# Layer 1's row statistics on ScalarE instead of VectorE, and an older split of the copies that prepare layer 0's weights

## The chip, the cores and the metric

The kernel runs on one core of one Trainium2 chip. Five engines of the core work side by side, each with its own instruction stream: TensorE (PE in the profile; PEld is its weight load), VectorE (DVE), ScalarE (ACT), GpSimd (POOL) and SyncE (SP, which here only issues DMAs). The metric is the device time of one execution in microseconds (us). The kernel before takes 5475.15 us, the median of three runs (5474.11 to 5475.48).

## What is computed

Four graph layers follow one another over a batch of 128 graphs with 128 nodes and 512 features; after each layer the input is added and every row is normalised. The change touches two of them. Cut to what matters:

```python
def _layernorm(x, axis=-1, eps=1e-5):
    m = jnp.mean(x, axis=axis, keepdims=True)
    v = jnp.var(x, axis=axis, keepdims=True)
    return (x - m) / jnp.sqrt(v + eps)

# layer 0 (its weights Wv, aw, Wk are prepared once, at the start of the kernel)
Xw = X @ Wv + bv
sj = Xw @ aw[:d, 0]
si = Xw @ aw[d:, 0]
...
for k in range(Wk.shape[0]):               # 3 steps
    H = H + Xk @ Wk[k] + bk[k]
    Xk = jnp.einsum('bij,bjd->bid', transition, Xk)

# layer 1: 128 graphs x 128 nodes, hidden width 1024
h = jax.nn.relu(hypergraph_conv(x, adj, W1, b1))     # rows of 1024
h = layer_norm(h, gamma, beta)                       # mean and variance of each row of 1024
y = hypergraph_conv(h, adj, W2, b2)
return y + x
```

Layers 2 and 3 (a tanh graph attention and an eight-head attention) are not touched.

## The kernel before

All the instructions of the kernel are first written into a plan. Each gets a key (the place in time it should have), an estimated duration and its dependences; a list scheduler in the host code then fixes the order of the instructions on every engine, and only then are they emitted. So every instruction has the same source line (L369) in the profile, and groups are told apart by tile names. The scheduler takes TensorE's instructions by key, and the others by the time at which TensorE needs them. An engine executes its instructions strictly in the order that was fixed, so a change of a few instructions gives a new order for everything behind it.

The weight products are two-level Strassen products: seven blocks for each of seven blocks. In layer 1 an inner product (`strassen` with `nk=1`) writes seven 256-column results, and each of them has to be read out of its PSUM bank before the bank is used on. Five of the seven inner products are read by VectorE alone (`biased_take`), two by ScalarE and VectorE (`plain_take`):

```python
def biased_take(dst, bias, scale=None):
    def op(d, b, u):
        if scale is None:
            return lambda p: ve.tensor_tensor(d, p, b, OP.add)
    ...
def plain_take(d11, d12, d21, d22):
    add = ve.tensor_tensor
    return {
        "p1": lambda p: ac.copy(d11, p), "c11": lambda p: add(d11, p, d11, OP.add),
        "v": lambda p: ac.copy(d12, p), "c12": lambda p: add(d12, p, d12, OP.add),
        "p5": lambda p: ac.copy(d22, p), "c22": lambda p: add(d22, p, d22, OP.add),
        "c21": lambda p: ac.copy(d21, p),
    }
```

The rows of 1024 are finished like this, once for each of the 128 graphs (128 partitions are the graph's nodes, 1024 elements lie along the free axis, in two halves `g`):

```python
def stats(st, k, piece):
    ve.bn_stats(st[:, 6 * k:6 * k + 6], piece)

def norm_terms(st, n=1):
    mv = col(2)
    ve.bn_aggr(mv, st[:, :6 * n])
    ve.tensor_scalar(mv[:, 1:2], mv[:, 1:2], EPS, None, op0=OP.add)
    ve.tensor_scalar(mv[:, 0:1], mv[:, 0:1], -1.0, None, op0=OP.mult)
    rstd = col(1)
    po.tensor_tensor(rstd, mv[:, 1:2], neghalf, OP.pow)
    nmr = col(1)
    ac.mul(nmr, mv[:, 0:1], rstd)
    return nmr, rstd
...
# in layer1, for each graph
ve.scalar_tensor_tensor(t, t, dns[r][b], rows1[:, :2]..., op0=OP.mult, op1=OP.add)
ac.activation(t, t, AF.Relu)
sts = col(12)
for g in range(2):
    stats(sts, g, h[r][b][:, g])
nmr, rstd = norm_terms(sts, 2)
ac.activation(t, t, AF.Identity, bias=nmr, scale=rstd)
loads.append(through_dram(...))     # written to DRAM and read back turned
```

`norm_terms` also serves the rows of 512 that end every layer; those are not changed.

The preparation of layer 0's weights, at the very start: the twelve transfers of `Wk`'s first half go through ScalarE's own DMA queue, Wv is transposed by TensorE, and the score columns `Wv @ aw` are taken from the transposed copy:

```python
for g in range(2):
    for m in range(3):
        with plan.together():
            for k in range(4):
                (ac, sp)[g].dma_start(stage[m]..., wk0[m]...)      # g=0: on ScalarE's queue
...
wvT = [four() for _ in range(2)]
for j in range(C):                                                 # C = 4
    pt = bank()
    ... pe.transpose(...) x4
    ve.tensor_copy(wvT[j // 2][:, j % 2]..., pt...)
two = fixed(C, 2, name="cols0")
p = bank()
... pe.matmul(p[:, 2 * c:2 * c + 2], wvT[...], awc...) x32         # Wv @ aw
ac.copy(two.rearrange("p c k -> p (c k)"), p[:, :2 * C])
for g, half, j in ((0, 0, B11), (1, 0, B21), (0, 1, B12), (1, 1, B22)):
    for m in range(3):
        (ac.copy, ve.tensor_copy)[g](W[j]..., stage[m]...)         # 128x512 each
    ...
    combine(W[j], (ve, po)[half])          # four subtractions of 386 columns
combine_once_more(W, (T3, N4))             # four subtractions of 2702 columns
```

Of the kernel before, what the change touches and what calls it, by code (L numbers as in the profile page):

```python
# [13 lines left out]
AF = mybir.ActivationFunctionType  # L14
OP = mybir.AluOpType
AX = mybir.AxisListType

P = 128
D = 512
C = D // P  # L20
Q = 32
DH = 1024
# [3 lines left out]
EPS = 1e-5  # L26
# [1 line left out]
BUFS = 12  # L28
SQS = 8
COLS = 32  # L30
ROWS = 4
KS = 4
OUTS = 4

# [343 lines left out]
def kernel(  # L378
# [57 lines left out]
    def fixed(*shape, name, kind="fixed"):  # L436
        t = const.tile([P, *shape], FP, name=name)
        return View(Tile(kind, t), np.arange(math.prod(shape)).reshape(shape))
# [11 lines left out]
    def col(*n):  # L450
        return tile_of("col", *n)
# [4 lines left out]
    neghalf = fixed(1, name="neghalf")  # L456
    po.memset(neghalf, -0.5)
    tiny = fixed(1, name="tiny")
    po.memset(tiny, 1e-12)
    junk = fixed(D, name="junk", kind="free")  # L460

    def dot(dst, u, v, n=D):
        ve.scalar_tensor_tensor(junk[:, :n], u, 1.0, v, op0=OP.mult, op1=OP.mult, accum_out=dst)
# [172 lines left out]
# [13 lines that stand above are left out]
# [164 lines left out]
    def prepare0():  # L813
        h = D // 2
# [27 lines left out]
        for j in range(C):  # L842
            pt = bank()
            with plan.together():
                for c in range(C):
                    pe.transpose(pt[:, c * P:(c + 1) * P], st[c // 2][:, c % 2, j * P:(j + 1) * P], ident)

            ve.tensor_copy(wvT[j // 2][:, j % 2].rearrange("p (c k a) -> p k c a", k=4, a=Q),
                                             pt.rearrange("p (k c a) -> p k c a", k=4, a=Q))
        two = fixed(C, 2, name="cols0")  # L850
        p = bank()
# [6 lines left out]
        ac.copy(two.rearrange("p c k -> p (c k)"), p[:, :2 * C])  # L858
        for g, half, j in ((0, 0, B11), (1, 0, B21), (0, 1, B12), (1, 1, B22)):
            for m in range(3):  # L860
                (ac.copy, ve.tensor_copy)[g](W[j][:, :4, :, m * P:(m + 1) * P].rearrange("p (n c) o i -> p c n (o i)", n=2), stage[m].rearrange("p c (n i) -> p c n i", i=P)[
                    :, 2 * g:2 * g + 2, 2 * half:2 * half + 2])
            scores = W[j][:, :4, 0, 3 * P:]
            if half:
                po.memset(scores, 0.0)
            else:
                po.memset(scores[:, 2:], 0.0)
                ac.copy(scores[:, :2], two[:, 2 * g:2 * g + 2])
            combine(W[j], (ve, po)[half])
        combine_once_more(W, (T3, N4))  # L870
        p = bank()
# [135 lines left out]
    def layer1(i0):  # L1007
# [66 lines left out]
        for r, i in enumerate(both):  # L1074
            plan.key = base + STEP1 * (5, 7)[r]
            for b in range(U):
                t = h[r][b].rearrange("p g f -> p (g f)")
                ve.scalar_tensor_tensor(t, t, dns[r][b], rows1[:, :2].rearrange("p g f -> p (g f)"),
                                        op0=OP.mult, op1=OP.add)
                ac.activation(t, t, AF.Relu)  # L1080
                sts = col(12)
                for g in range(2):
                    stats(sts, g, h[r][b][:, g])
                nmr, rstd = norm_terms(sts, 2)
                ac.activation(t, t, AF.Identity, bias=nmr, scale=rstd)
                loads.append(through_dram(h[r][b].rearrange("p (j g) (k w) -> p j (g k) w", j=1, k=2), f"h{i + b}"))
        for r, i in enumerate(both):
# [296 lines left out]
```

## Time and profile before

| | |
|---|---|
| span of the profiled execution | 5473.7 us |
| instructions | 94041 |
| TensorE busy | 5349.7 us (98%) |
| VectorE busy | 4551.0 us (83%) |
| GpSimd busy | 4041.0 us (74%) |
| ScalarE busy | 2392.4 us (44%) |
| two DVE groups on the rows of 1024: statistics of one half, aggregation | 681 ns, 199 ns mean |

How to read it. Busy shares are averages over the whole span; the layers lie one behind the other and have different limits, so the shares of a stretch say more than these. "Idle before" of a group is the time that its engine stood still just before the group's instructions, with the engine whose instruction ended most of it. The tile names tell the use: `bank` and `t` are PSUM, `first` is the large area that holds layer 0's weights at first and the rows of 1024 in layer 1 (128x1024, or 128x512 for a half), `col` the small per-row numbers.

### The profile page before, as it was taken

To read this page: it belongs to the slowest core of one execution; us is meant where nothing else is said; L and a number is where in the kernel's file an instruction comes from. 1 tells how busy PE (TensorE), PEld (TensorE's weight loads), DVE (VectorE), ACT (ScalarE), POOL (GpSimd) and SP (SyncE) were. 2 spreads that over 40 slices of the span, in tenths; PEclk is the share of its full clock that TensorE was granted. 3 is DMA by queue.
4 is the path that set the end of the run, shared out by engine and by line. 5 is a ranking of instruction groups with operands and counts; after the bars stand their busy time and mean duration, and the time that the engine had idled before them with its cause. 6 is when DMAs were issued, how large, how long until landed. Compare 5 with 4: busy or idle time off the path is not lost.

```text
span 5473.7 us, 94041 instructions
## 1 busy us (share of the span) xinstructions
PE 5349.7 (98%) x29145; PEld 4259.2 (78%) x29145; DVE 4551.0 (83%) x11561; ACT 2392.4 (44%) x6471; POOL 4041.0 (74%) x4835
## 2 busy tenths in 40 slices
PE   8999999999999999999999999999999999999998
PEld 4555555555788888888888789999999999999987
DVE  6788888878998899998889978778878777878876
ACT  2444343434434434443434344444455445445444
POOL 6666666666777777877777567777777777777776
PEclk8999999999999999999999999999999999999999
DMA  3333333334454545545445545554555554555553
GB/s 93 104 98 98 101 101 102 94 103 129 145 150 144 155 144 148 155 148 152 147 148 150 161 129 165 161 162 154 162 162 156 162 163 151 162 166 159 160 154 119
DMA packets 788381, 768.35 MB, mean 140 GB/s; under 512 B 264859, under 2 KB 592547, under 8 KB 787878
## 3 DMA queue, kind: packets, MB, share of 16 engines
q1 hardware_dynamic: 786374, 759.71, 45.8%
q8 instruction: 231, 3.78, 0.3%
q10 hardware_dynamic: 1504, 2.62, 0.2%
q14 instruction: 272, 2.23, 0.1%
HBM read 435.83 MB, written 326.24 MB: 139 GB/s over the span
## 4 chain that ended last, share of the span: by engine, by line
PE 57%; DVE 7%; DMA 3%; POOL 1%; issue 1%; ACT 1%; SPq 1%; DVEq 0%; POOLq 0%; ACTq 0%
PE bank L369 43%; PE t L369 15%; DVE first L369 2%; DVE col L369 2%; DVE out L369 1%; DVE four L369 1%; SPq L369 1%; POOL out L369 1%; DMA h<-first 1%; DMA out<-h 1%; ACT first L369 0%; DVE junk L369 0%; DMA first<-x3d 0%; POOL first L369 0%; POOL four L369 0%
## 5 line engine op out<-in xcount | busy, mean ns | idle before, releaser
L369 PE MATMUL bank<-first,four 128*128 128x386 f32 (+3 forms) x5176 | 1437.1, 431 | 37.2 <-DVE out L369 14.8
L369 PEld LDWEIGHTS bank<-first,four 128*128 128x128 f32 (+2 forms) x5176 | 847.7, 187 | 592.9 <-DVE out L369 139.0
L369 DVE TENSOR_TENSOR out<-bank,out 128x386 f32<-128x386 f32 (+1 forms) x1884 | 928.1, 510 | 282.4 <-PE bank L369 223.3
L369 POOL TENSOR_TENSOR out<-out 128x256 f32<-128x256 f32 (+3 forms) x482 | 550.4, 1152 | 300.6 <-DVE out L369 210.0
L369 POOL TENSOR_TENSOR col<-col,neghalf 128x1 f32<-128x1 f32 x640 | 380.6, 600 | 377.8 <-DVE col L369 376.2
L369 DVE TENSOR_TENSOR first<-bank,first 128x256 f32<-128x256 f32 x1362 | 543.6, 414 | 130.2 <-PE bank L369 100.6
L369 PE MATMUL bank<-first,out 128*128 128x256 f32 (+2 forms) x2560 | 624.0, 382 | 26.4 <-DVE first L369 9.4
L369 PEld LDWEIGHTS bank<-first,out 128*128 128x128 f32 (+1 forms) x2560 | 469.2, 190 | 128.7 <-DVE first L369 30.8
L369 PE MATMUL bank<-four,out 128*128 128x256 f32 (+2 forms) x2118 | 538.4, 376 | 2.2 <-DVE col L369 1.4
L369 DVE TENSOR_TENSOR four<-bank,four 128x256 f32<-128x256 f32 x818 | 338.4, 418 | 142.1 <-PE bank L369 127.5
L369 PE MATMUL bank<-out,first 128*128 128x128 f32 (+2 forms) x2840 | 427.9, 290 | 0.9 <-DVE out L369 0.4
L369 ACT COPY out<-bank 128x258 f32<-128x258 f32 (+2 forms) x555 | 236.7, 431 | 436.8 <-PE bank L369 388.6
L369 PEld LDWEIGHTS bank<-four,out 128*128 128x128 f32 (+2 forms) x2118 | 369.8, 189 | 58.5 <-issue 8.4
L369 PEld LDWEIGHTS bank<-out,first 128*128 128x128 f32 (+1 forms) x2840 | 374.5, 188 | 24.7 <-DVE four L369 2.8
L369 ACT ACTIVATE col<-col,col 128x1 f32<-128x1 f32 x640 | 183.2, 292 | 456.4 <-POOL col L369 388.2
L369 POOL TENSOR_TENSOR four<-four,four 128x256 f32<-128x256 f32 (+2 forms) x395 | 328.8, 837 | 14.4 <-DVE col L369 4.8
L369 ACT COPY t<-out 128x512 f32<-128x512 f32 x256 | 150.2, 591 | 421.1 <-DVE four L369 248.8
L369 POOL TENSOR_TENSOR first<-first 128x512 f32<-128x512 f32 (+3 forms) x196 | 234.4, 1208 | 105.5 <-DVE first L369 67.4
L369 POOL TENSOR_TENSOR four<-four 128x256 f32<-128x256 f32 (+2 forms) x331 | 245.4, 758 | 66.9 <-DVE four L369 36.3
L369 POOL TENSOR_TENSOR out<-out,out 128x256 f32<-128x256 f32 (+2 forms) x286 | 287.2, 1008 | 9.3 <-DVE four L369 4.5
L369 POOL TENSOR_SCALAR sq<-sq,col 128x128 f32<-128x128 f32 x256 | 160.7, 638 | 148.8 <-DVE col L369 146.5
L369 DVE BATCH_NORM_STATS2 col<-first 128x6 f32<-128x512 f32 x370 | 245.7, 681 | 26.9 <-ACT first L369 25.1
(407 smaller groups left out, 12718.5 us busy)
## 6 DMA issues: line engine op xcount, KB each, us to landing
h<-first SPq DMA_DIRECT2D x496, 128.0 KB, 2.4
out<-x1d SPq DMA_DIRECT2D x88, 512.0 KB, 4.5
out<-h SPq DMA_DIRECT2D x87, 512.0 KB, 4.6
four<-in_x_dram SPq DMA_DIRECT2D x512, 64.0 KB, 2.0
four<-in_x_dram SPq DMA_DIRECT2D x62, 512.0 KB, 3.6
x1d<-four SPq DMA_DIRECT2D x62, 512.0 KB, 2.7
first<-S SPq DMA_DIRECT2D x61, 512.0 KB, 4.4
out<-S SPq DMA_DIRECT2D x50, 512.0 KB, 4.4
```

The lines of the kernel that those rows point to most:

```text
L369: call(*map(real, args), **{n: real(a) for n, a in kw.items()})
```

## The change

Layer 1's rows get their mean from the accumulator that the relu can write as it goes, and their variance from two squares on ScalarE, each of which also writes the sum along its half. With `mean` holding minus the sum over 32 times 1024, a square computes (h/32 + mean) squared, so that the two sums together are the variance. Three small VectorE instructions make the numbers from these, and the product of mean and factor moves from ScalarE to VectorE. VectorE's statistics and their aggregation fall away for these rows. The purpose is to take work off VectorE in layer 1.

The same diff takes back an arrangement in the preparation of layer 0's weights: two of the four copies of the transposed Wv go from VectorE to ScalarE, and so do six copies of Wk's blocks. The pool of rows of 512 is cut from four buffers to two, which makes room for a scratch tile for the squares' outputs.

```diff
-ROWS = 4
+ROWS = 2
...
+    junk_act = fixed(D, name="junk_act", kind="free")
...
-            ve.tensor_copy(wvT[j // 2][:, j % 2].rearrange("p (c k a) -> p k c a", k=4, a=Q),
+            (ve.tensor_copy, ac.copy)[j % 2](wvT[j // 2][:, j % 2].rearrange("p (c k a) -> p k c a", k=4, a=Q),
...
-                (ac.copy, ve.tensor_copy)[g](W[j][:, :4, :, m * P:(m + 1) * P]...
+                ac.copy(W[j][:, :4, :, m * P:(m + 1) * P]...
...
-                ac.activation(t, t, AF.Relu)
-                sts = col(12)
+
+                total, mean, var, rstd, nmr = col(1), col(1), col(2), col(1), col(1)
+                ac.activation(t, t, AF.Relu, accum_out=total)
+                ve.tensor_scalar(mean, total, -1 / (32 * DH), None, op0=OP.mult)
                 for g in range(2):
-                    stats(sts, g, h[r][b][:, g])
-                nmr, rstd = norm_terms(sts, 2)
+                    ac.activation(junk_act, h[r][b][:, g], AF.Square, bias=mean, scale=1 / 32, accum_out=var[:, g:g + 1])
+                ve.tensor_scalar(var[:, :1], var[:, :1], var[:, 1:], EPS, op0=OP.add, op1=OP.add)
+                po.tensor_tensor(rstd, var[:, :1], neghalf, OP.pow)
+                ve.tensor_scalar(nmr, mean, rstd, 32.0, op0=OP.mult, op1=OP.mult)
                 ac.activation(t, t, AF.Identity, bias=nmr, scale=rstd)
```

More of the change, by code (lines that the diff above doesn't have):

```diff
@@ L860, in prepare0 @@
             for m in range(3):
-                (ac.copy, ve.tensor_copy)[g](W[j][:, :4, :, m * P:(m + 1) * P].rearrange("p (n c) o i -> p c n (o i)", n=2), stage[m].rearrange("p c (n i) -> p c n i", i=P)[
+                ac.copy(W[j][:, :4, :, m * P:(m + 1) * P].rearrange("p (n c) o i -> p c n (o i)", n=2), stage[m].rearrange("p c (n i) -> p c n i", i=P)[
                     :, 2 * g:2 * g + 2, 2 * half:2 * half + 2])
```

## The prediction

> **What bounds the kernel now.** I read the page's busy shares first, then busy time in windows of 100 us to find the layers, then the waits of TensorE inside layer 1, then single groups, and last the timeline of the first 60 us. TensorE is busy 98% of the span, so the question is only where its last 2% lie. Layer 1 runs from about 1330 to 3100 us (the writes of its rows to DRAM start at 1386 us and end at 3101); layers 2 and 3 come behind it. Two windows, one in the middle of layer 1 and one in the middle of layers 2 and 3; the columns are length, then busy us of each engine with its instructions, clock, DMA share and GB/s:
>
> ```profile
> core 0: us, PE busy (x) PEld busy (x) DVE busy (x) ACT busy (x) POOL busy (x), PEclk, DMA share, GB/s
> 1300.00:1500.00 200.00, 183.15 (x820) 140.95 (x821) 186.80 (x457) 82.11 (x161) 155.84 (x188) 0.97 0.51 151
> 1500.00:3000.00 1500.00, 1472.56 (x7027) 1238.26 (x7026) 1353.46 (x3362) 610.71 (x1149) 1162.87 (x1360) 1.00 0.50 148
> 3300.00:5200.00 1900.00, 1896.86 (x14099) 1734.50 (x14096) 1522.96 (x4036) 943.02 (x3222) 1479.21 (x1820) 1.00 0.52 160
> ```
>
> In layers 2 and 3 VectorE is busy 80% (1522.96 of 1900), ScalarE 50%, GpSimd 78%, and TensorE stands still for 3.1 us of 1900. In layer 1 VectorE is busy 90%, ScalarE 41%, GpSimd 78%, and TensorE stands still for 27.4 us of 1500. The entry, 1300 to 1500, loses another 16.9 us with VectorE at 93%. What TensorE waits for in 1500 to 3000 (total us, times, longest), matmuls and weight loads:
>
> ```profile
> PE bank L369 <- DVE col L369: 11.4, 11, 2.0
> PE bank L369 <- DVE first L369: 6.7, 15, 0.9
> PE t L369 <- DVE col L369: 3.1, 3, 1.8
> PE t L369 <- DVE first L369: 2.8, 8, 0.7
> PE bank L369 <- ACT four L369: 2.3, 3, 0.9
> ```
>
> ```profile
> PEld bank L369 <- DVE first L369: 38.1, 77, 1.3
> ```
>
> 24.0 of the 26.9 us of matmul waits are ended by VectorE: late evictions (`first`) and work queued in front of them (`col`). The weight loads wait for VectorE far oftener, 77 times here and 34 times (16.8 us) into the other PSUM tiles, in pieces of 0.5 us in the mean; part of each is hidden by the matmul still running. So layer 1 is TensorE-bound with VectorE close behind, and VectorE's queue is what ends TensorE's pauses.
>
> **What the Trainium skill says.** "Perfetto Trace Analysis", Identifying the Most-Contended Engine, says that matmul busy time is no good measure of how near TensorE is to its limit. The trace agrees: stretches of layer 1 that all read 97 to 99% busy do 459 to 480 matmuls in 100 us. I therefore use the count as well. "ScalarE: Activation LUTs", What ACT_TABLE_LOAD costs, gives an ACTIVATE with a pointer bias about 280 ns + 0.833 ns per element, with 93 ns of overlap between neighbours. The slope agrees here: (1240 - 813) / 512 = 0.834 ns from the Identity on 1024 and on 512 columns. The same page, Table sets: the hidden batching unit, says that a function outside the loaded set needs a reload; the trace has one table load (1283 ns) in the whole kernel, and no run yet shows a Square. "GPSIMD Engine Reference", Specifications, says that GpSimd shares its SBUF interfaces with VectorE and collides with VectorE instructions of two SBUF inputs. The statistics have one input, so taking them away should shorten GpSimd's work little. The collision itself is in the trace: the 128x1024 scalar_tensor_tensor takes from 1220 to 4655 ns.
>
> **The change part by part.** The groups of 1500 to 3000 give VectorE's costs (busy us, mean ns), and a stretch of layer 3's timeline gives the spacing of activations that write a sum:
>
> ```profile
> L369 DVE BATCH_NORM_STATS2 col<-first 128x6 f32<-128x512 f32 x218 | 143.0, 681 | 22.6 <-ACT first L369 22.3
> ...
> L369 DVE TENSOR_SCALAR col<-col 128x1 f32<-128x1 f32 x440 | 48.9, 143 | 1.5
> ...
> L369 DVE BATCH_NORM_AGGREGATE col<-col 128x2 f32<-128x12 f32 x110 | 21.9, 199 | 1.1
> ```
>
> ```profile
> 4022.76 0.41 ACT L369 ACTIVATE first<-first,col 128x128 f32<-128x128 f32 x1
> 4023.05 0.21 ACT L369 ACTIVATION_READ_ACCUMULATOR first<-first,col 128x1 f32 x1
> 4023.15 0.41 ACT L369 ACTIVATE first<-first,col 128x128 f32<-128x128 f32 x1
> ```
>
> VectorE, per graph. Removed: two statistics of 143.0/218 = 0.656 us, one aggregation of 0.199, two small instructions of 48.9/440 = 0.111, together 1.73 us. Added: three small instructions, two of them with pointer operands; I take 0.14 us each, 0.42 us. Net -1.31 us, times 128 graphs -168 us. Spread over the 1770 us of layer 1 that is 9.5 points, so VectorE goes from 90% to about 81%.
>
> ScalarE, per graph. An activation of 128 columns with its sum follows the last after 0.39 us; 384 further columns at 0.834 ns make 0.32, so a Square of 512 costs about 0.71 us, two 1.42. The relu's sum costs the part of the read that doesn't overlap, 4023.15 minus 4023.05, 0.10. The product for nmr goes, 0.29 (its mean is 292 ns). Net +1.23 us, times 128 is +157 us, 9 points: ScalarE from 41% to about 50%.
>
> GpSimd keeps its one power per row. The latency of one row changes little: 1.3 us of statistics become 1.4 us of squares, and a step through VectorE is added where one through ScalarE is removed. It has slack anyway: the plan wants a row's statistics between 1.1 and 1.5 steps into the stage and its read-back at 2.4 to 3.0, and one step is 28 us (1770 / 64).
>
> After the change layer 1 has the same shares as layers 2 and 3 have now (VectorE 80%, ScalarE 50%, GpSimd 78%), whose inner products have the same seven evictions. That is my main ground: TensorE's idle time per 100 us should fall from 1.8 us towards the 0.17 us there. By the count, the best undisturbed 100 us of layer 1 (2100 to 2200) holds 480 matmuls; 7027 at that rate would take 1464 us in place of 1500, so 36 us are to be had there, 42 us over 1770. I take 60% of that, 25 us, since some of the stalls come from the mixture of work and from the order rather than from load. At the entry (16.9 us idle, VectorE 93%) about 10 us are ended by VectorE; I take 4 of them, because layer 1's first rows come only late in it.
>
> The preparation, from the timeline of the first microseconds (start, length, engine; idle before in brackets):
>
> ```profile
> 11.02 4.65 PEld L369 LDWEIGHTS bank<-aw_c,four 128*128 128x128 f32 x32
> ...
> 17.47 1.28 ACT L369 ACT_TABLE_LOAD   x1 [17.47 <-DMA first<-in_L_gnn_Wk_dram]
> ...
> 22.03 0.16 ACT L369 COPY cols<-bank 128x8 f32<-128x8 f32 x1
> ...
> 22.23 1.84 DVE L369 TENSOR_TENSOR first<-first 128x386 f32<-128x386 f32 x2 [8.84 <-ACT cols L369]
> ```
>
> ScalarE issues DMAs until 17.4 us and can compute only from 18.8. The two Wv copies that move to it were done on VectorE by 11.1 us; there they end at about 20. The 32 score products (4.7 us) then run from 20 to 24.7, the copy of the columns comes at 24.8 in place of 22.03, and VectorE's first subtraction is some 2.7 us later. Against it, VectorE loses six Wk copies, 1.22 + 0.88 + 1.33 = 3.4 us, in a stretch (20 to 40 us) where it is busy 17.4 of 20 and sets TensorE's pauses, and ScalarE, busy 4 of 20, has room for them. I book 0, give or take 3.
>
> The row pool has four users in the whole kernel, and the later two start long after the first two have ended: 0. Sum: -25 - 4 + 0 = -29, and a point of pessimism for the reordering of stages that already lose almost nothing. 5475 - 28 = 5447 us.
>
> **The rivals.** First: ScalarE becomes the new late one. In layer 1 it evicts 22 results per four graphs, and an eviction that arrives behind two squares and an Identity waits 1.4 + 1.24 us. Against it: layers 2 and 3 run rows of eight exponentials (over 3 us without a break) at the same load with TensorE idle 0.17%. For it: 2.3 us of waits on `ACT four` exist already at 41%. If it holds, half of the gain is lost: 5460 us.
>
> Second: the stalls aren't VectorE's load but its order. An eviction is due about 0.4 us after its matmul, and any 1.2 to 1.7 us instruction in front of it (transposes, scalar_tensor_tensor) makes it late; the statistics at 0.66 us are the smaller obstacles. Then only their share counts: perhaps 10 us, 5465 us.
>
> Third: the new order, with nothing of the mechanism, moves other stages by chance. Layer 0 (from 100 to 1200 us) idles 4 us in all and layers 2 and 3 scarcely, so they can only lose; I give this 10 us either way.
>
> Fourth: Square needs a table reload. Layer 1 uses only Relu, Identity, Copy and Square, so one set could serve throughout it, and the cost would be a few loads at the borders, under 10 us; only alternating loads would cost hundreds, and I give that 1%.
>
> **Range and chances.** The centre is 5447. Full success (42 + 10, with a lucky preparation) makes 5423, the first two rivals 5460 to 5465, with the third on top 5475. I take 5430 to 5466 for eight in ten. A gain of 2% would be 109 us, more than twice what layer 1 loses, so it needs something I don't see: 1.5%. A loss of 2% needs table reloads or a broken order: 1%.
>
> **What would show it.** In the windows of layer 1 VectorE near 81%, ScalarE near 50%, TensorE's idle time under 10 us in 1500 of its middle, and more than 475 matmuls per 100 us; the waits on `DVE first` and `DVE col` more than halved; in ScalarE's groups 256 Squares of about 0.7 us busy and still one table load; the score columns copied near 24.8 us but layer 0 at full pace at about the same time as before. I am wrong if the VectorE waits shrink and ScalarE's grow by as much (first rival), or if VectorE falls to 81% and its waits stay (second), or if the time moves outside layer 1.

## The result, and the profile after

| | median us | runs (lowest to highest) | ratio to before, 95% interval |
|---|---|---|---|
| before | 5474.63 | 4 (5472.12 to 5475.48) | |
| after | 5506.34 | 4 (5496.10 to 5514.32) | 1.0058 [1.0038, 1.0077] |

The change costs 31.7 us where I predicted a gain of 28. The profiled run is the fastest of the four; its span is 5494.3 us, so the trace accounts for 20.6 of these 31.7 us and is silent on the rest.

First the busy times in windows, the same columns as before. The third window is the passage from layer 1 to layer 2.

```profile
core 0: us, PE busy (x) PEld busy (x) DVE busy (x) ACT busy (x) POOL busy (x), PEclk, DMA share, GB/s
1300.00:1500.00 200.00, 180.01 (x811) 139.37 (x811) 171.74 (x438) 93.40 (x198) 156.08 (x186) 0.95 0.48 146
1500.00:3000.00 1500.00, 1465.43 (x7014) 1238.30 (x7012) 1269.88 (x3131) 755.91 (x1588) 1178.97 (x1360) 1.00 0.50 148
3000.00:3300.00 300.00, 273.52 (x1534) 232.69 (x1535) 249.29 (x590) 126.95 (x333) 183.53 (x208) 0.97 0.49 151
3300.00:5200.00 1900.00, 1890.20 (x14000) 1720.49 (x13998) 1513.64 (x4005) 925.21 (x3182) 1470.38 (x1807) 1.00 0.52 158
```

The relief is there: in the middle of layer 1 VectorE falls from 90.2% to 84.7% and ScalarE rises from 40.7% to 50.4%. TensorE doesn't profit. It stands still for 34.6 us in place of 27.4 and gets 7014 matmuls done in place of 7027. And in layers 2 and 3, which the change doesn't touch, 14000 matmuls fit where 14099 did; at their pace of 7.42 a microsecond that is 13 us.

What TensorE's matmuls wait for between 1500 and 3000 us (total us, times, longest):

```profile
PE bank L369 <- ACT first L369: 29.0, 26, 1.2
PE bank L369 <- DVE first L369: 1.9, 5, 0.5
PE t L369 <- DVE first L369: 1.7, 3, 0.8
```

VectorE ended 24.0 us of these waits before and ends 3.6 now. In their place stands one wait that wasn't there, for ScalarE, 26 times with some 1.1 us each: once in every group of four graphs (layer 1 has 32 such groups, and this window holds about 27). The timeline around one of them, with start, length and engine; I left out what lies between:

```profile
1998.83 0.72 ACT L369 ACTIVATE junk_act<-first,col 128x512 f32<-128x512 f32 x1
...
1999.68 0.72 ACT L369 ACTIVATE junk_act<-first,col 128x512 f32<-128x512 f32 x1
...
2002.13 0.20 DVE L369 TENSOR_SCALAR col<-col,col 128x1 f32<-128x1 f32 x1
...
2002.38 1.24 ACT L369 ACTIVATE first<-first,col,col 128x1024 f32<-128x1024 f32 x1 [1.88 <-DVE col L369]
...
2002.85 1.77 DVE L369 SCALAR_TENSOR_TENSOR four<-rows,col 128x512 f32<-128x512 f32 x1
...
2004.54 0.15 DVE L369 TENSOR_SCALAR col<-bank 128x2 f32<-128x2 f32 x1
...
2004.72 0.38 ACT L369 COPY ks<-bank 128x260 f32<-128x260 f32 x1 [0.85 <-DVE col L369]
...
2005.00 0.38 ACT L369 COPY first<-bank 128x256 f32<-128x256 f32 x1
...
2005.52 0.67 PE L369 MATMUL bank<-first,out 128*128 128x256 f32 x2 [1.03 <-ACT first L369]
```

Read it from the bottom. TensorE stops for 1.03 us because the eviction at 2005.00 came late. ScalarE wasn't busy then: it stood at the head of its queue with a copy of K (`ks<-bank`), the node-by-node product of two of layer 1's graphs, which waits for VectorE to read the same PSUM bank first (`col<-bank`), and VectorE was held up by a scalar_tensor_tensor of 1.77 us. Before that, ScalarE had waited 1.88 us for `nmr`, which the change moved from ScalarE to VectorE. So this isn't load but waiting at the head of an in-order queue. ScalarE's waits show how common it is (total us, times, longest); before, `first` waited for VectorE's small results 22.6 us and `ks` 10.6, and there was no `junk_act`:

```profile
ACT first L369 <- DVE col L369: 68.5, 54, 1.9
ACT junk_act L369 <- DVE col L369: 45.2, 54, 1.4
ACT ks L369 <- DVE col L369: 43.7, 41, 2.0
```

The costs of the added instructions, ScalarE's and then VectorE's groups of the same window (busy us, mean ns | idle just before):

```profile
L369 ACT ACTIVATE junk_act<-first,col 128x512 f32<-128x512 f32 x220 | 158.9, 722 | 48.8 <-DVE col L369 45.2
L369 ACT ACTIVATE first<-first,col,col 128x1024 f32<-128x1024 f32 x109 | 135.5, 1243 | 58.9 <-DVE col L369 57.5
...
L369 ACT ACTIVATION_READ_ACCUMULATOR junk_act<-first,col 128x1 f32 x220 | 41.1, 187 | 0.0
```

```profile
L369 DVE TENSOR_SCALAR col<-col 128x1 f32<-128x1 f32 x440 | 64.1, 161 | 48.1 <-ACT first L369 30.7 <-ACT junk_act L369 14.7
```

The preparation and the passage to layer 2, from the timeline:

```profile
19.52 6.71 PE L369 MATMUL bank<-aw_c,four 128*128 128x2 f32 x30 [6.30 <-ACT four L369]
...
26.27 0.17 ACT L369 COPY cols<-bank 128x8 f32<-128x8 f32 x1 [4.24 <-PE bank L369]
...
3140.19 1.23 DVE L369 STREAM_TRANSPOSE out<-four 128x1024 f32<-128x1024 f32 x1
...
3141.53 2.05 PE L369 MATMUL bank<-first,out 128*128 128x256 f32 x4 [12.88 <-issue]
```

The score columns come at 26.27 us; I had expected 24.8. At 3141 TensorE has stood for 12.9 us; the profile names nothing that ended this wait, but VectorE's transpose into `out` ended just before it. Almost all of it comes back: against the same matmul of the kernel before, after lags by 5.9 us at matmul 12100, 15.7 at 12200 and 5.7 at 12700.

To see where time goes I compare two traces by TensorE's matmuls done: when was the n-th finished? Matmul 3500 ends at 1208 us of the kernel before, ahead of layer 1; 13000 at 3276 us, behind the passage to layer 2; 28500 at 5369 us. After lags by 2.2 us at the first, 6.3 at the second, 21.9 at the third. So the preparation and layer 0 cost 2.2 us, layer 1 with its passage 4.2 (I had predicted -29), and layers 2 and 3 cost 15.5 (I had predicted 0).

### The profile page after: what moved, and what is told of

Read it like the earlier page. It is cut to its first block, busy times and chain, and to the rows that moved or that the text cites. A ratio compares the mean times of both kernels' runs of the same rounds, so it can differ in the third digit from the quotient of the medians.

```text
span 5494.3 us, 94155 instructions
## 1 busy us (share of the span) xinstructions
PE 5347.4 (97%) x29145; PEld 4258.8 (78%) x29145; DVE 4451.9 (81%) x11297; ACT 2559.9 (47%) x6991; POOL 4059.3 (74%) x4835
## 4 chain that ended last, share of the span: by engine, by line
PE 55%; DVE 9%; DMA 4%; ACT 2%; issue 2%; SPq 2%; POOL 1%; DVEq 0%; ACTq 0%; POOLq 0%
PE bank L369 42%; PE t L369 12%; DVE out L369 3%; DVE first L369 2%; DVE col L369 2%; SPq L369 2%; DVE four L369 1%; ACT first L369 1%; DMA out<-x1d 1%; DMA out<-h 1%; DMA sq<-in_adj_dram 1%; ACT junk_act L369 1%; DVE junk L369 0%; DMA out<-x3d 0%; DMA four<-x1d 0%
## 5 line engine op out<-in xcount | busy, mean ns | idle before, releaser
L369 PE MATMUL bank<-first,four 128*128 128x386 f32 (+3 forms) x5184 | 1497.9, 437 | 23.4 <-DVE out L369 10.9
L369 PE MATMUL bank<-first,out 128*128 128x256 f32 (+2 forms) x3214 | 770.4, 379 | 51.5 <-ACT first L369 29.5
L369 PEld LDWEIGHTS bank<-first,out 128*128 128x128 f32 (+1 forms) x3214 | 585.3, 189 | 174.0 <-issue 65.7
L369 DVE TENSOR_TENSOR four<-bank,four 128x256 f32<-128x256 f32 x1094 | 447.8, 417 | 203.2 <-PE bank L369 189.6
L369 DVE TENSOR_TENSOR first<-bank,first 128x256 f32<-128x256 f32 x1179 | 477.0, 415 | 130.1 <-PE bank L369 93.2
L369 POOL TENSOR_TENSOR first<-first 128x512 f32<-128x512 f32 (+4 forms) x237 | 250.7, 1069 | 185.5 <-DVE first L369 146.4
L369 PE MATMUL bank<-four,out 128*128 128x256 f32 (+2 forms) x1354 | 343.4, 372 | 2.7 <-DVE first L369 1.7
L369 POOL TENSOR_TENSOR four<-four 128x256 f32<-128x256 f32 (+1 forms) x342 | 244.9, 734 | 61.4 <-DVE four L369 40.7
L369 ACT COPY four<-bank 128x256 f32<-128x256 f32 (+1 forms) x245 | 108.8, 448 | 330.2 <-PE bank L369 323.5
L369 PE MATMUL t<-out,sq 128*128 128x512 f32 x512 | 259.9, 595 | 0.6 <-DVE sq L369 0.4
L369 PEld LDWEIGHTS bank<-four,out 128*128 128x128 f32 (+2 forms) x1354 | 228.4, 185 | 41.1 <-DVE first L369 10.3
```

The lines of the kernel that those rows point to most:

```text
L369: call(*map(real, args), **{n: real(a) for n, a in kw.items()})
```

## The experiments

The plan's own part in this has to be told first. It orders everything once, and then up to twice more with deadlines taken from the order before; I call what it writes after one and after two of these steps the first and second order. It keeps the one with the earlier end by its own estimate. For the kernel before these ends are 5363.67 and 5364.69 us and it emits the first order; for after 5359.26 and 5356.73, and it emits the second. So a change of a few instructions also switches the order of 94,000, on an estimate that is 0.05% lower.

Theory A is that the loss lies in the change itself: its row statistics pass between the queues of the engines seven times (VectorE, ScalarE, VectorE, ScalarE, VectorE, GpSimd, VectorE, ScalarE) where they passed four times, and every pass is a chance to block a queue. Theory B is that the order decides. Theory C is ScalarE's load, theory D the preparation.

All 18 runs, and the change itself, in one table. Each ratio is to the kernel before as it was measured again beside that run; its medians there lay between 5473.7 and 5479.6 us, so medians of runs that were not measured together compare only to some 5 us. "Layer 1" is what a run gains (-) or loses against the kernel before between matmul 3500 and matmul 13000, "layers 2, 3" between 13000 and 28500, each from one profiled run; e1, which does in layer 1 what after does, differs from after by 2 and 1 us there, so differences of a few us say nothing. Ahead of matmul 3500 the runs lag by -1 to 10 us, which is in neither column.

| run | median us | ratio, 95% interval | layer 1 | layers 2, 3 |
|---|---|---|---|---|
| after | 5506.3 | 1.0058 [1.0038, 1.0077] | +4.2 | +15.5 |
| e1 after, old preparation | 5506.0 | 1.0053 [1.0038, 1.0068] | +6.5 | +16.9 |
| e2 before, new preparation | 5479.8 | 1.0003 [0.9995, 1.0012] | -1.5 | -0.2 |
| e3 after, first order | 5472.2 | 0.9992 [0.9983, 1.0001] | -14.2 | +3.8 |
| e4 before, second order | 5491.7 | 1.0028 [1.0019, 1.0038] | -4.1 | +13.5 |
| e5 after, K copy later | 5527.8 | 1.0093 [1.0078, 1.0108] | +29.9 | +16.2 |
| e6 after, no squares, first order | 5480.6 | 1.0006 [0.9999, 1.0012] | -5.4 | +6.6 |
| e7 before, third order | 5493.4 | 1.0028 [1.0017, 1.0040] | -6.2 | +21.7 |
| e8 after, third order | 5500.2 | 1.0044 [1.0029, 1.0059] | +8.1 | +17.1 |
| e9 after, K copy sooner | 5498.0 | 1.0036 [1.0024, 1.0049] | +2.7 | +20.3 |
| e10 after, one SBUF input | 5505.1 | 1.0043 [1.0030, 1.0055] | +10.6 | +18.3 |
| e11 before, slack 50 | 5469.5 | 0.9983 [0.9975, 0.9990] | -23.4 | +11.0 |
| e12 after, slack 50 | 5489.6 | 1.0021 [1.0015, 1.0028] | -5.7 | +11.2 |
| e13 no pass through VectorE | 5458.4 | 0.9973 [0.9962, 0.9984] | -21.4 | +1.5 |
| e14 the same, slack 50, second order | 5487.1 | 1.0023 [1.0014, 1.0031] | -11.4 | +15.7 |
| e15 before, nmr on VectorE | 5477.3 | 1.0007 [0.9999, 1.0015] | -1.1 | +0.4 |
| e16 one VectorE step | 5497.2 | 1.0039 [1.0025, 1.0053] | +8.9 | +13.6 |
| e17 e13 in the second order | 5469.7 | 0.9985 [0.9978, 0.9991] | -24.5 | +17.7 |
| e18 e13, slack 50, first order | 5502.3 | 1.0043 [1.0029, 1.0057] | +14.4 | +9.2 |

**e1 and e2: which half of the change.** e1 is after with the preparation of before, e2 is before with the preparation of after and the smaller row pool.

```diff
 # e1
-            (ve.tensor_copy, ac.copy)[j % 2](wvT...
+            ve.tensor_copy(wvT...
-                ac.copy(W[j]...
+                (ac.copy, ve.tensor_copy)[g](W[j]...
 # e2: the same lines the other way round in before, and ROWS = 2
```

> The changed kernel with the preparation of the kernel before: only layer 1's statistics are moved. If the preparation's copies carry the loss, this is at or below 5475 us. If the loss comes from layer 1 and what follows (the main theory: VectorE's waits are gone, 24 us, but one wait of about 1.1 us on ScalarE for each of the 32 groups of four graphs, 35 us, has come in their place), it stays near the changed kernel, 5490 to 5512 us, with the start some 2 us earlier.

> The kernel before with only the preparation (and the row pool of 2) of the changed one. Lag at the start of the full pace in the changed kernel was about 2 us, so if nothing else depends on it 5477 us; if the preparation carries the loss, 5490 us or more.

Measured: e1 at 1.0053 loses all that after loses, e2 at 1.0003 nothing that can be told from zero. Theory D is out.

**e3 and e4: the same work in the other order.**

```diff
 # e3, in after: one step of deadlines
-    def emit(self, places, rounds=2):
+    def emit(self, places, rounds=1):
 # e4, in before: always take the later order
-            if other[2] < end:
+            if True:
```

> The changed kernel, but the plan emits its first order by deadlines and not the second one, which it took since its own estimate was lower by 0.05%; the kernel before was emitted in its first one. The instructions are the same ones. If the loss is the order's (what happens to stand in front of what), the time moves by more than 10 us, perhaps below 5475; if it is the work's (Squares on ScalarE), it stays within 5 us of the changed kernel and the waits on ScalarE in layer 1 stay at about 29 us in 1500 to 3000.

> The kernel before in its second order by deadlines, which it had turned down (its own estimate was higher by 0.02%). If orders of the same work differ by tens of us, this moves by more than 10 us; if the order matters little, 5475 within 5 us.

Measured: after in the first order takes 5472 us, 34 less than the same instructions in the second, so the whole loss is gone with the work unchanged. TensorE's waits for ScalarE's `first` in 1500 to 3000 are 4.0 us there in place of 29.0, the longest 0.3. Before in the second order takes 5492, 17 more. The windows of e4, in the middle of layer 1 and of layers 2 and 3:

```profile
1500.00:3000.00 1500.00, 1473.14 (x7035) 1240.56 (x7034) 1344.31 (x3368) 611.67 (x1148) 1170.99 (x1359) 1.00 0.50 149
3300.00:5200.00 1900.00, 1891.90 (x13995) 1719.73 (x13994) 1510.47 (x3999) 925.36 (x3184) 1469.26 (x1804) 1.00 0.52 159
```

In the second line the old work loses the same hundred matmuls (13995 against 14099) as after did, with the shares of the engines hardly changed: what after lost in layers 2 and 3 is the order's and not the change's. The matmuls' own waits there are only 8.1 us; the weight loads show the rest of it in part. The four largest groups of their waits for VectorE come to 10.9 us in before in this stretch, and to 28.9 us in e4:

```profile
PEld bank L369 <- DVE out L369: 14.2, 38, 1.6
PEld bank L369 <- DVE four L369: 7.0, 30, 0.6
PEld bank L369 <- DVE first L369: 5.0, 13, 1.1
PEld bank L369 <- DVE ks L369: 2.7, 10, 1.1
```

**e5 and e9: is the copy of K what blocks ScalarE's queue?** Both take after's order and move only this copy. e5 issues it behind the two evictions that follow; some of the copies then read a bank that the next product had overwritten, which changes the numbers but not the work. e9 issues it in front of VectorE's read of the same bank.

```diff
-        for k in sorted(range(len(start)), key=...):
+        for k in self.k_later(sorted(range(len(start)), key=...)):            # e5
+        for k in self.k_sooner(sorted(range(len(start)), key=...), place):    # e9
```

> The changed kernel in its own (second) order, with one thing moved: ScalarE's copy of K out of PSUM, which stands behind a VectorE instruction that reads the same bank, goes behind the two evictions that TensorE waits for. Theory (that copy, waiting for VectorE, blocks ScalarE's queue and so makes the evictions late, 29 us in 1500 to 3000, about 33 in all of layer 1): the waits on ACT first in 1500 to 3000 fall from 29 to under 6 us and the time falls from about 5506 by 20 to 33 us. Rival (the Squares and the Identity in front of them make the evictions late): waits and time stay within 8 us.

> The changed kernel in its own (second) order, with every engine's sequence as it is, but ScalarE's copy of K is issued in front of VectorE's first read of the same PSUM bank, so that VectorE waits for ScalarE there and not ScalarE for VectorE. In the changed kernel 62 of the 64 copies of K wait for VectorE; here 5 do. If that wait is what makes ScalarE's evictions late: TensorE's waits on ACT first in 1500 to 3000 fall from 29 us to under 8, and the time falls by 15 to 30 us, to 5475 to 5490. If the Identity and the Squares in front do it: no change within 6 us.

Measured: e5 was a miss. The copy now stood behind a later VectorE read of the bank, where it waited 1.46 us in every second group of graphs (0.80 in the others) in place of 0.85, and in front of other evictions. TensorE's wait for ScalarE stayed (31.5 us, 26 times), and the kernel lost some 20 us more. In e9 every engine's queue holds the same instructions in the same order as in after, but for five of ScalarE's 6991 places; what differs is who waits for whom at this bank. Of the 64 copies 47 wait for a semaphore of VectorE in after, and 3 in e9. What TensorE waits for in e9 between 1500 and 3000 (the line number differs, since the helper is longer):

```profile
PE bank L400 <- DVE first L400: 14.0, 35, 0.7
PE t L400 <- DVE first L400: 3.1, 8, 0.6
PE bank L400 <- ACT first L400: 3.1, 13, 0.2
```

The wait for ScalarE fell from 29.0 to 3.1 us, which shows that the blocked copy caused it. But half of it came back as waits for VectorE (17.1 us against 3.6), in 43 pieces of at most 0.7 us, and the weight loads' waits for VectorE's `first` doubled (57.5 us against 28.2). TensorE's idle time fell from 34.6 to 23.0 us, yet it did 7022 matmuls in the window in place of 7014, and layer 1 costs 2.7 us in place of 4.2. The median is 8 us lower, with intervals that overlap, where I had expected 15 to 30. So the blocked copy is what TensorE was seen to wait for; that it is what layer 1 lost isn't shown.

**e6: theory C, ScalarE's load.** Without the squares; the variance's place is taken by a number without meaning, so the rows get another scale; the squares are all that is left out. First order, to be compared with e3.

```diff
-                for g in range(2):
-                    ac.activation(junk_act, h[r][b][:, g], AF.Square, bias=mean, scale=1 / 32, accum_out=var[:, g:g + 1])
-                ve.tensor_scalar(var[:, :1], var[:, :1], var[:, 1:], EPS, op0=OP.add, op1=OP.add)
+                ve.tensor_scalar(var[:, :1], total, mean, EPS, op0=OP.add, op1=OP.add)
```

> The changed kernel in the plan's first order, without the two Squares (a number made of the row's sum stands for the variance, so the rows are scaled wrongly): VectorE is relieved and ScalarE gets nothing for it. If the Squares on ScalarE take away part of the gain, this is well under the changed kernel's first order (5472), 5460 or less. If the gain is bounded by how evictions stand in VectorE's queue, it is within 6 us of 5472.

Measured:

```profile
1500.00:3000.00 1500.00, 1479.75 (x7073) 1245.89 (x7073) 1242.53 (x3160) 595.99 (x1154) 1143.16 (x1371) 1.00 0.51 150
```

ScalarE falls to 39.7%, below what it had before the change, and VectorE is at 82.8%. Yet TensorE still idles 20.3 us, and the run is not faster than e3, which does all the squares (1.0006 against 0.9992). As the cause of the loss, theory C is out. Since e6 too has an order of its own, an effect of ScalarE's load smaller than the tens of us between orders can't be excluded. And with VectorE relieved and ScalarE not burdened at all, layer 1 gains 5 us: relief alone wasn't worth 29 here.

**e7, e8, e11, e12: two further orders of both kernels.** The third order takes three steps of deadlines; the slack is a constant of the plan's scheduler.

```diff
-    def emit(self, places, rounds=2):
+    def emit(self, places, rounds=3):      # e7 before, e8 after; the last order is always taken
-SLACK = 60
+SLACK = 50                                 # e11 before, e12 after; both plans take the first order
```

> The kernel before in its third order by deadlines. The first gave 5477 and the second 5492. A third value some 10 us from either would show that an order is worth as much as the change; together with the changed kernel's third order it gives a third pair that differs in the work alone.

> The changed kernel in its third order by deadlines. If the change of work is worth 10 to 15 us in layer 1 as in the first order, 10 to 15 us under the kernel before in its third order; if the Squares cost as much as the statistics did, equal or above, and waits on ScalarE in layer 1 of 20 us or more come back.

> The kernel before with the plan's slack at 50 in place of 60 (how far ahead of the readiest instruction it may pick by rank): the same instructions in one more order. By the three orders so far, 5477 to 5493.

> The changed kernel with the slack at 50: a fourth pair. If the change itself is worth the 4 us of the first pair, it is near the kernel before with this slack, within 8 us; if the new waits on ScalarE go with the change in most orders, as in two of three, it is 7 to 30 us above.

Measured: in pairs of the same setting, after against before is -0.08% (first), +0.30% (second), +0.16% (third) and +0.38% (slack 50), in the ratios of the table. The change loses in three orders of four; the first pair can't be told apart. In layer 1 alone, by the table, it is worth -14, +8, +14 and +18 us in these pairs, so the sign is the order's. The most telling run is e11, which has the old statistics on VectorE:

```profile
1500.00:3000.00 1500.00, 1484.24 (x7106) 1251.86 (x7106) 1346.95 (x3388) 621.23 (x1160) 1178.83 (x1380) 1.00 0.50 150
```

VectorE is as busy as before, 89.8%, and TensorE does 7106 matmuls in place of 7027 and idles 15.8 us in place of 27.4. Layer 1 gains 23 us, most of what I had meant to win by relieving VectorE, with no relief at all. Of the changed kernel's orders, e8 has the once-per-group wait for ScalarE again (25.7 us, 23 times). In e12 such a wait is there, too, but on the other engine:

```profile
PE bank L369 <- DVE first L369: 27.3, 25, 1.9
```

**e10: does a collision of VectorE and GpSimd start the stall?** The 1.77 us instruction that held up VectorE in the timeline adds b2 from a second SBUF operand. e10 leaves that addition out and reads one operand (the form it uses also writes a sum, which adds a read of some 0.08 us).

```diff
+                if self.ops[k][0] == DVE and ...:     # rows * factor + b2
+                    nc.vector.tensor_scalar(to, u, s, None, op0=OP.mult, op1=OP.add, accum_out=spare)
```

> The changed kernel in its own order, but VectorE's product of bw2 and the row number, 128x512, doesn't add b2 (which is zero), so it has one SBUF input and can't collide with GpSimd: 0.99 us should become about 0.65 us. At the place of the wait it stretches to 1.77 us beside GpSimd's 128x512 subtractions, in front of VectorE's read of K's bank. If that delay starts the chain (VectorE late, ScalarE's copy of K late, eviction late), TensorE's waits on ACT first fall from 29 us to under 12 and the time by 15 to 30 us. If it doesn't, within 8 us of the changed kernel.

Measured: 1.0043, and the wait for ScalarE is still 26.3 us, 26 times. But the delay has only moved. The two instructions that stand in front of VectorE's read of K's bank took 0.68 and 1.77 us in after (2002.26 and 2002.85); at such a place of e10 they are

```profile
2005.29 1.58 DVE L372 SCALAR_TENSOR_TENSOR four<-out,four 128x512 f32<-128x512 f32 x1
2006.79 0.73 DVE L1364 TENSOR_SCALAR_CACHE_REDUCE four<-rows,col 128x512 f32<-128x512 f32 x1
```

The changed instruction takes 722 to 748 ns throughout e10, whatever GpSimd does. Its neighbour, which still has two SBUF operands (`four<-out,four` and `out<-out,out`), takes up to 687 ns where GpSimd stands still, and 1311 ns in the mean, up to 1797, where GpSimd works all the while. So the collision is real, and e10 didn't take it away; whether it starts the stall stays open.

**e13, e14, e17, e18: theory A by itself.** All row statistics on ScalarE and GpSimd, with no pass through VectorE between the relu and the Identity: one square over 1024 elements, and the factor 32 that is left over goes into W2.

```diff
-                ve.tensor_scalar(mean, total, -1 / (32 * DH), None, op0=OP.mult)
-                for g in range(2):
-                    ac.activation(junk_act, h[r][b][:, g], AF.Square, bias=mean, scale=1 / 32, accum_out=var[:, g:g + 1])
-                ve.tensor_scalar(var[:, :1], var[:, :1], var[:, 1:], EPS, op0=OP.add, op1=OP.add)
-                po.tensor_tensor(rstd, var[:, :1], neghalf, OP.pow)
-                ve.tensor_scalar(nmr, mean, rstd, 32.0, op0=OP.mult, op1=OP.mult)
+                ac.mul(mean, total, -1 / DH)
+                ac.activation(junk_act, t, AF.Square, bias=mean, accum_out=var)
+                ac.activation(var, var, AF.Identity, bias=eps1)          # eps1 holds 1024 * EPS
+                po.tensor_tensor(rstd, var, neghalf, OP.pow)
+                ac.mul(nmr, mean, rstd)
```

The plan takes the first order for it at slack 60 (e13) and the second at slack 50 (e14). e17 and e18 are the two that are missing: second order at 60, first at 50.

> The changed kernel with the whole of layer 1's row statistics off VectorE: ScalarE also scales the sum, squares all 1024 columns in one instruction, adds eps and forms nmr (rows stay a factor of 32 small, W2 is loaded 32 times larger). A row then goes VectorE, ScalarE, GpSimd, ScalarE, and VectorE's queue holds nothing that waits for ScalarE. ScalarE does about as much as in the changed kernel. Theory A (VectorE's queue is held up by small instructions that wait for ScalarE and GpSimd, 55 us in 1500 to 3000 of the changed kernel against 22 before, and evictions stand behind them): VectorE's waits for ScalarE and GpSimd in the chain are gone, layer 1 gains 15 us or more on the kernel before, the time is 5450 to 5465. Theory B (layer 1 loses by the order alone): anything between 5465 and 5500, with a wait once in each group of four graphs.

> The same work as the last with the plan's slack at 50, another order, to be held against the kernel before with that slack (5469) and the changed kernel with it (5490). Theory A: 10 us or more under the kernel before, 5445 to 5460. Theory B: no steady sign against the other kernels.

> The row statistics wholly on ScalarE and GpSimd, as in the run of 5458 us, but in the plan's second order (the one that the changed kernel has). If the passages between the engines' queues cost the changed kernel its gain, this one beats it in the same order by 10 to 20 us in layer 1, as it did in the first order (14 us): 5485 to 5497 us, about the 5492 of the kernel before in its second order or below. If only the order counts, it comes out where the changed kernel is: 5500 to 5512.

> The same statistics with the other slack (50 for 60), but in the plan's first order, as the kernels before and after with that slack have it (5469 and 5490 us); the 5487 us measured of it were in the second order. If the passages count: below the changed kernel's 5490 by 15 us or more, so 5455 to 5475. If only the order counts, anything from 5470 to 5490, with no gain in layer 1 beyond that of the changed kernel.

Measured: e13 takes 5458.4 us and beats both kernels, 0.27% below before [0.9962, 0.9984]. ScalarE's groups show that the waiting for VectorE in front of squares and Identity is gone (48.8 and 58.9 us of idle time in after's lines above, next to 3.5 and 0.9 here):

```profile
L369 ACT ACTIVATE first<-first,col,col 128x1024 f32<-128x1024 f32 x110 | 136.1, 1237 | 0.9
L369 ACT ACTIVATE junk_act<-first,col 128x1024 f32<-128x1024 f32 x110 | 126.4, 1149 | 3.5
```

e17 speaks for theory A most clearly. In the second order the version without the passes takes 5469.7 us, where after takes 5506.3 and before 5491.7; that is more than I expected of it. Its windows:

```profile
1500.00:3000.00 1500.00, 1475.37 (x7086) 1251.79 (x7087) 1232.88 (x2838) 790.17 (x1701) 1135.63 (x1379) 1.00 0.51 150
...
3300.00:5200.00 1900.00, 1890.63 (x13980) 1716.68 (x13979) 1512.08 (x4002) 925.21 (x3183) 1471.62 (x1807) 1.00 0.52 159
```

Layer 1 gains 24 us, and layers 2 and 3 lose what every second order loses. But e18 is a miss, and it limits what theory A may claim. (So is e14, with 5487 us where theory A had 5445 to 5460; no run has the old work or the change in its order.) The same work without passes, at slack 50, takes 5502 us, more than after (5490) and before (5469) there. Its waits of TensorE in 1500 to 3000:

```profile
PE bank L369 <- ACT four L369: 22.9, 22, 1.7
PE bank L369 <- DVE first L369: 18.1, 17, 2.1
```

New waits again, more than one per group of graphs, half of them for ScalarE's copies into another area (`four`) than that of the rows, half for VectorE.

**e15 and e16: one pass more, one pass fewer.** e15 is before with only `nmr` moved to VectorE, as the change does. e16 is after with mean and nmr on ScalarE, so that one VectorE step is left.

```diff
 # e15
-        ac.mul(nmr, mv[:, 0:1], rstd)
+        ve.tensor_scalar(nmr, mv[:, 0:1], rstd, None, op0=OP.mult)     # rows of 1024 only
 # e16
-                ve.tensor_scalar(mean, total, -1 / (32 * DH), None, op0=OP.mult)
+                ac.mul(mean, total, -1 / DH)
-                ve.tensor_scalar(nmr, mean, rstd, 32.0, op0=OP.mult, op1=OP.mult)
+                ac.mul(nmr, mean, rstd)
```

> The kernel before, with VectorE's statistics as they are, but nmr of the rows of 1024 formed on VectorE instead of ScalarE: one more passage from GpSimd to VectorE to ScalarE, 128 small instructions of about 0.2 us. Theory A: VectorE waits for GpSimd inside the chain, and the time rises by 5 to 15 us, to 5482 to 5492. If such a passage costs nothing but its instruction: 5475 to 5480.

> Between the changed kernel and the first of this call: two Squares of 512 as in the change, but the scaled sum and nmr on ScalarE, so that one VectorE instruction (the sum of the two halves) is left in a row's chain in place of three. The changed kernel is 5506, the kernel before 5477. Theory A: 5460 to 5485. Theory B: by chance, 5465 to 5506.

Measured: e15 has the new wait in a smaller form,

```profile
PE bank L369 <- ACT first L369: 15.6, 26, 0.8
```

but its time is that of before (1.0007), since the waits for VectorE shrank as well. e16, with four passes, as many as before, isn't clearly better than after (1.0039 [1.0025, 1.0053] against [1.0038, 1.0077]); its plan takes the second order, too, in which layer 1 gains 4 us with the old work (e4) and loses 9 in e16. Neither supports theory A by its time.

**What follows.** That the loss is the order's is shown: e3 takes it away with the same instructions. In layers 2 and 3, whatever the work, the first orders at slack 60 stand at 0 to +7 us (before, e2, e3, e6, e13, e15), the second and third at +13 to +22 (after, e1, e4, e5, e7 to e10, e16, e17), and those at slack 50 at +9 to +16; which instructions of an order do it there isn't shown. For layer 1 two things are shown: that after's once-per-group wait is a queue blocked at its head (in e9 one copy no longer waits for VectorE's read, and the wait goes, though layer 1 gets back hardly more than 1 us), and that VectorE's share of busy time doesn't set the time (e11, with e6 as the other side of it). That the passes are the general reason is supported by e13 and e17, contradicted by e18, and not supported by e14, e15 and e16. That passes and order act together, so that a pass costs something only where the order puts urgent work behind it, is how I read these runs; none of them shows it by itself. Why the layout of e18 loses 14 us in layer 1 where that of e17 gains 24 stays open; I have no run that changes one place of e18's order alone.

## Why the prediction was wrong

What it had right. TensorE is the bound, and its pauses in layer 1 were ended by VectorE: those waits fell from 24.0 to 3.6 us, more than halved as asked. ScalarE's share came out at 50.4% for "about 50%". No second table load came. The smaller row pool and the preparation were 0, give or take 3: e2 says +0.03%. There I carried the 4.65 us of the score products' weight loads over from before; the products take 6.71 us in after, so the columns came at 26.27 in place of 24.8, and still layer 0 never lags by more than 3.8 us and ends with 2.2. Of the signs of being wrong that I had named, two came: TensorE's waits for ScalarE grew by more than those for VectorE shrank (29.0 us came, 20.4 went), and most of the lost time lies outside layer 1.

What failed, in the order of size:

1. The main ground, "after the change layer 1 has the same shares as layers 2 and 3 have now", so that "TensorE's idle time per 100 us should fall from 1.8 us towards the 0.17 us there". It equates busy shares with idle time. In after VectorE came down to 84.7%, and TensorE's idle time rose from 27.4 to 34.6 us. Layer 1 in e11 idles 15.8 us at 90% of VectorE, and e6 idles 20.3 us at 83% and an unburdened ScalarE. So the stalls depend on where single instructions stand in the queues. My second rival, "the stalls aren't VectorE's load but its order", came nearest. I gave it 10 us of gain, and 5 to 14 is what the relief brings in layer 1 in the first order (e6: -5.4, e3: -14.2). But I looked only at VectorE's queue, and at no order in which the change loses.

2. "The latency of one row changes little ... It has slack anyway." I counted "a step through VectorE" for one through ScalarE, where the passes between queues go from four to seven, and I counted the row's latency and not what a wait does to the queue in which it stands. A row with slack may wait; the eviction behind it on ScalarE may not. ScalarE's waits for VectorE's small results grew as the lines above show. The new wait of 29.0 us on TensorE is one for an eviction, as the first rival foresaw, but not by load ("behind two squares and an Identity"): it came from a blocked copy of K (e9). How much of the missing gain this step explains stays open, since e9 removes the wait and gains little, and e18 loses without the passes.

3. "They can only lose; I give this 10 us either way", of layers 2 and 3 under a new order. They lost 15.5 us, and orders of the same instructions differ by 34 us for after (5472 to 5506), 24 for before (5469 to 5493) and 44 for the version of e13 (5458 to 5502). The term was of the size of the whole expected gain and should have set the width of the range: with it, something like 5430 to 5510 (an estimate from these differences).

4. The sizes. VectorE was relieved by 83.6 us in 1500, over 110 rows 0.76 us each and not 1.31; statistics and aggregation fell away as computed, but the row's small instructions came to 37.2 us more (64.1 and 22.0 us in place of 48.9), 0.34 us per row where I had 0.20, and most of the rest went to the neighbours: a tensor_scalar of 128x2 took 538 ns in place of 215 (17 us together), and the 128x512 scalar_tensor_tensors 892 ns in the mean in place of 849. A square of 512 with its sum comes every 0.85 us (1998.83 to 1999.68) and not every 0.71: the whole read of 0.187 us with some overlap is paid, where I took the spacing of activations of 128 columns for granted. Neither size explains the result: e6, without the squares, is no faster than e3.

The Trainium skill was cited on the contention of engines ("Perfetto Trace Analysis") for preferring counts to busy time, and that held: in e4 TensorE's busy time differs from before by 5.0 us in 1900 (1896.86 to 1891.90), its count by 104 matmuls or 14 us. On collisions ("GPSIMD Engine Reference", Specifications) e10 agrees: beside GpSimd, VectorE's instructions with two SBUF inputs were stretched (687 ns at most alone, 1311 in the mean beside it) and those with one were not (748 ns at most).

## What to carry to other kernels

Where a host-side plan orders all instructions anew, a small change is measured together with a new order: first run the old work in some other orders (here 24 us apart), and compare changes in matched orders, or the best of each (here 5469 us for the old work, 5472 for the change, 5458 without the passes through VectorE). Before moving work to an engine with room, count how often the chain then passes between in-order queues (e13 and e17 speak for this, e18 against it as the only measure), and look what urgent instruction, an eviction above all, stands behind each place where it is waited for. And the free share of an engine doesn't tell whether relieving another will pay: look whether a late instruction was late because its engine was busy or because it waited at the head of its queue.

## What the runs showed of the hardware that I had not expected

ScalarE's copy out of a PSUM bank was released by VectorE's read of the same bank where that had been issued earlier: the copy waited 0.85 us in after, 0.80 or 1.46 when it was issued behind a still later read (e5), and only 3 of the 64 copies waited for a semaphore of VectorE where they were issued first (e9). Since the queues of e9 hold the same order as those of after, the wait comes from the semaphores that the program sets between the two readers, in the order of issue. Whether the two reads could run at the same time no run here shows.

A square over 1024 elements takes 1.149 us with one read of the accumulator, two over 512 take 0.72 us and a read of 0.19 us each: one long activation is cheaper than two halves by about a third of a microsecond (2 x 0.85 = 1.70 us against 1.149 + 0.187 at most).
